# Layer 1 of a graph network: one head's product as an exponential of logs for eight row tiles in 32 instead of four, with adj added by GpSimd

## The chip, the cores and the metric

The kernel runs on one core of one Trainium2 chip. The metric is the device time of the whole program in microseconds. The kernel before took 2879.15 us (median of three runs, 2877.86 to 2881.1). In what follows TensorE is PE in the profile, VectorE is DVE, ScalarE is ACT, GpSimd is POOL and SyncE is SP; "us" is a microsecond.

## What is computed

The network has two layers over 4096 nodes with 512 features. Layer 0 (an attention with adj as mask) isn't touched. Layer 1, which the change touches, is a graph attention with 8 heads of 64 features; its connectivity is adj itself, added to the scores:

```python
data1 = (data @ W.T + b).reshape(N, H, D)            # N = 4096, H = 8, D = 64
src = jnp.einsum('nhd,xhd->nh', data1, src_proj)
trg = jnp.einsum('nhd,xhd->nh', data1, trg_proj)
e = src.T[:, :, None] + trg.T[:, None, :]
e = jnp.where(e >= 0, e, 0.01 * e)
e = e + connectivity[None, :, :]                     # adj, 0 or 1
scores = jax.nn.softmax(e, axis=-1)
out = jnp.einsum('hnm,hmd->hnd', scores, data1.transpose(1, 0, 2))
```

An unnormalised weight is thus exp(leaky(s + t)) times exp(adj). With the leaky slope 0.01, exp(leaky(s + t)) is the larger of two products of a factor of the column (from s) and one of the row (from t). The softmax is divided by its row sums at the end.

## The kernel before

**Layout.** Layer 1 holds the weights transposed: partitions are m (the neighbours, 32 row tiles of 128, NT = 32), the free dimension is n in blocks of WL = 1024 columns (two halves of BL = 512). A *group* i is one block of columns and one set of four heads, HG = 4: eight groups in all. A *step* is one row tile m of one group: 256 steps. For each step and each of the four heads k a tile pr of 128x1024 float32 is made, and TensorE multiplies it with the values.

**The stages.** The order of all work is written out by hand (line 1317 and the loop behind it): in step s each stage is called for the step that lies so many steps ahead, and each engine runs its instructions in the order in which they are issued.

- `load`, 4 ahead: SyncE loads the adj tile e (four buffers). At certain m it also loads the column factors z of the next group, and at m = 28 the column row u of the next group.
- `exps`, 1 ahead: ScalarE writes ex = exp(adj) into PSUM, one buffer (line 1061).
- `weigh`, 1 ahead: VectorE makes the products in the order 3, 0, 1, 2. Heads 1 and 2 (line 1107) and head 0 (line 1104) read ex from PSUM; head 3 (line 1107 too) reads e3 from SBUF. GpSimd adds product 3 onto the sum acc3 (line 1116) and, for the row tiles in BY_DMA, issues a DMA that adds product 0 onto one of two sums acc0 (line 1122).
- `factors`, 2 ahead: ScalarE writes e3 = exp(adj + log factor of the row) (line 1071), and for head 0 the Relu part rl (line 1089) from which VectorE's line 1104 makes the larger of the two products.
- `logs`, 0 ahead, before: see below.
- `scale`, 2 ahead, in the first two groups alone: GpSimd, later ScalarE (line 1057), scales the values by factors of the rows.
- `gather`, 0 ahead: TensorE's matmuls of the step (lines 1139 and 1144): 32 with the values and 8 for the row sums of heads 1 and 2. For a row tile that is not in BY_DMA TensorE also sums product 0 (line 1144 with zo). `side` counts these row tiles, and turns the order of the two halves of the array. At the last row tile the sums acc0 and acc3 are added up, and ScalarE copies the four results out of PSUM (line 1172).
- Behind the stages, at the steps in PARTS, a part of `finish` for the group before: transposes on TensorE, the reciprocal on VectorE, copies with a scale on ScalarE (line 1225), and a DMA that adds x on GpSimd's queue (line 1230). In group 0 this place belongs to `tables`.

**Head 0 by logs.** For the four row tiles in BY_LOG head 0's product takes another way, which needs no VectorE instruction: ScalarE makes lg = Relu of the column row u (line 1078), a DMA from GpSimd's queue adds adj from HBM onto it (line 1079), and ScalarE writes pr0 = exp(lg + log of the row) (line 1086). The dictionary says at which step lg is made: row tile 10 in step 5, 16 in 10, 22 in 16, 27 in 22. The exponential stands in `factors`, in place of that row's Relu of line 1089, and VectorE then has three products in the row's step. lg has one buffer, pr0 has three, the other products have two, rl two.

Of the kernel before, what the change touches and what calls it, by code (L numbers as in the profile page):

```python
# [8 lines left out]
FP = mybir.dt.float32  # L9
AF = mybir.ActivationFunctionType  # L10
ALU = mybir.AluOpType
# [4 lines left out]
P = 128  # L16
# [3 lines left out]
SLOPE = 0.01  # L20


def row_bcast(ap, n, offset=0):

    return bass.AP(tensor=ap.tensor, offset=ap.offset + offset, ap=[[0, P], [1, n]])
# [3 lines left out]
def kernel(  # L29
# [15 lines left out]
    nc = tc.nc  # L45
    N, F = x.shape
    H, D = 8, 64
    HG, WL = 4, 1024
    WT = WL // P
    NT = N // P  # L50
    KC = F // P
    BL = 512
# [12 lines left out]
    u_d = dram.tile([2, NT, P], FP, name="u_d")  # L65
# [20 lines left out]
    t_m = big.tile([P, H, NT], FP, name="t_m")  # L86
# [6 lines left out]
    rl = s_n.rearrange("p h t -> p (h t)").rearrange("p (t b) -> p t b", b=NB)  # L93
# [11 lines left out]
    with tc.tile_pool(name="w0", bufs=1) as wp, tc.tile_pool(name="a0", bufs=2) as ap_, tc.tile_pool(  # L105
        name="a0s", bufs=8
# [355 lines left out]
    with tc.tile_pool(name="mx", bufs=1) as mxp, tc.tile_pool(name="b_a", bufs=6) as adjp, tc.tile_pool(  # L462
        name="b_e", bufs=1
    ) as esp, tc.tile_pool(name="b_m", bufs=4) as mkp, tc.tile_pool(name="b_s", bufs=2) as sp, tc.tile_pool(
        name="b_p", bufs=6, space=PSUM
# [11 lines left out]
        def load(i, j, t):  # L477
            w, lo, sk = parts(i, j, t)
            rows = slice(t * P, (t + 1) * P)
            ar = adjp.tile([P, BL], FP, name="ar")  # L480
            nc.sync.dma_start(ar[:, :w], adj[rows, lo:lo + w])
            ac = adjp.tile([P, BL], FP, name="ac")
            nc.sync.dma_start(ac[:, :w], adj_t[rows, lo:lo + w])
            loaded[i, j, t] = ar, ac
# [36 lines left out]
        for n in range(-6, len(items)):  # L521
# [3 lines left out]
            if n >= 0:  # L525
                i, j, t = items[n]
# [17 lines left out]
    with tc.tile_pool(name="c_a", bufs=7) as adjp, tc.tile_pool(name="c_e", bufs=9) as etp, tc.tile_pool(  # L544
        name="c_d", bufs=5
    ) as wkp, tc.tile_pool(name="c_t", bufs=2) as atp, tc.tile_pool(name="c_u", bufs=2) as smp, tc.tile_pool(
        name="c_m", bufs=2
    ) as mxp, tc.tile_pool(name="c_o", bufs=4) as iop, tc.tile_pool(name="c_v", bufs=1) as cvp, tc.tile_pool(
        name="c_s", bufs=2
# [49 lines left out]
        def exps(b, m):  # L599
            if m == 0:  # L600
                mb = bank("m")
                nc.scalar.copy(mb, blk[b][0])
                blk[b][0] = mb
            mb, d, e, n = blk[b][0], ex[b, m], src.pop((b, m)), turned(b, m)
            if n:
                nc.vector.tensor_tensor(d[:, 0:n], d[:, 0:n], mb[:, 0:n], ALU.subtract)
            if n < BL:
                nc.vector.tensor_tensor(d[:, n:], e[:, n:], mb[:, n:], ALU.subtract)  # L608
            nc.scalar.activation(d, d, AF.Exp)  # L609
# [68 lines left out]
        left, scale, norms, joins = [], {}, iter(()), iter(())  # L678
# [191 lines left out]
        def gather(b, m):  # L870
# [5 lines left out]
            elif b:  # L876
                products(b - 1, NT // 2 - 1, PR[NF:])

        stages = ((load, 11), (load_a, 7), (gather, 0), (turn, 5), (exps, 4), (more_sums, 1), (weigh, 2), (sums, 2),
                  (residuals, 0))  # L880
        z = bank(PR[-1])
        pc = column_maxima(acc_z, z)
        dens = iter(())
        for s in range(-11, end):
            b, m = divmod(s, NT)
# [61 lines left out]
    nlg_m = l1.tile([P, H // HG, NT], FP, name="nlg_m")  # L947
# [26 lines left out]


    PARTS = (0, 1, 2, 3, 4, 6, 7, 8, 11, 12, 13, 18, 19, 20, 22)
    BY_LOG = {10: 5, 16: 10, 22: 16, 27: 22}
    BY_DMA = [m for m in range(NT) if m not in (4, 7, 13, 14, 19, 23, 24, 25, 29, 31)]

    with tc.tile_pool(name="p", bufs=2) as prp, tc.tile_pool(name="rl", bufs=2) as rlp, tc.tile_pool(  # L980
        name="io1", bufs=2
    ) as iop, tc.tile_pool(name="s1", bufs=1) as sp, tc.tile_pool(name="za", bufs=1) as zp0, tc.tile_pool(name="e3", bufs=2) as e3p, tc.tile_pool(
        name="zb", bufs=1
    ) as zp1, tc.tile_pool(name="e", bufs=4) as ep, tc.tile_pool(name="ac", bufs=2) as acp, tc.tile_pool(
        name="os", bufs=1
    ) as osp, tc.tile_pool(name="u", bufs=1) as usp, tc.tile_pool(
        name="p_x", bufs=1, space=PSUM
    ) as p_x, tc.tile_pool(name="p_v", bufs=1, space=PSUM) as p_v, tc.tile_pool(
        name="p_t1", bufs=1, space=PSUM
    ) as p_t, tc.manual_schedule():  # L990
        groups = [(b, g) for b in range(N // WL) for g in range(H // HG)]
        steps = [(i, m) for i in range(len(groups)) for m in range(NT)]
        us = {}
        zs_, ra, ex, e3, rl, pr, acc, pv, late = {}, {}, {}, {}, {}, {}, {}, {}, {}
# [35 lines left out]
        def zload(i, k):  # L1030
            b, g = groups[i]
            zs_[i, k] = (zp1 if i % 2 else zp0).tile([P, WL], FP, name=f"z{k}")
            nc.sync.dma_start(zs_[i, k], row_bcast(z_d, WL, (g * HG + k) * N + b * WL))

        def load(i, m):
            b, g = groups[i]
            e = ep.tile([P, WL], FP, name="e")
            nc.sync.dma_start(e, adj_t[m * P:(m + 1) * P, b * WL:(b + 1) * WL])
            ra[i, m] = e
            if i + 1 < len(groups) and m == 28:  # L1040
                us[i + 1] = usp.tile([P, WL], FP, name="u")
                b, g = groups[i + 1]
                nc.sync.dma_start(us[i + 1], row_bcast(u_d, WL, g * N + b * WL))
            m0, n = (3, 2) if i else (22, 1)
            if i + 1 < len(groups) and m0 <= m < m0 + HG // n:
                for k in ORDER[n * (m - m0):n * (m - m0) + n]:
                    zload(i + 1, k)

        def scale(i, m):


            if i < H // HG:
                for h in range(groups[i][1] * HG + 1, groups[i][1] * HG + 3):
                    if m < (6, 3)[i]:
                        nc.gpsimd.tensor_scalar(va[:, m, h, :], va[:, m, h, :], d_m[:, h, m:m + 1], None, ALU.mult)
                    else:
                        nc.scalar.activation(va[:, m, h, :], va[:, m, h, :], AF.Copy, scale=d_m[:, h, m:m + 1])

        def exps(i, m):
            x_ = p_x.tile([P, WL], FP, name="ex")  # L1060
            nc.scalar.activation(x_, ra.pop((i, m)), AF.Exp)  # L1061
            ex[i, m] = x_

        def factors(i, m):
            last_exps(i, m)
            relus(i, m)
# [4 lines left out]
            nc.scalar.activation(x_, ra[i, m], AF.Exp, bias=ld_m[:, h // HG, m:m + 1])  # L1071
            e3[i, m] = x_

        def logs(i, s):
            for m in [m for m in BY_LOG if BY_LOG[m] == s]:
                b, g = groups[i]
                r = rlp.tile([P, WL], FP, name="lg", bufs=1)
                nc.scalar.activation(r, us[i], AF.Relu, bias=nlg_m[:, g, m:m + 1], scale=-(1.0 - SLOPE))
                nc.gpsimd.dma_start(r, adj_t[m * P:(m + 1) * P, b * WL:(b + 1) * WL], accum_op=ALU.add)
                rl[i, m] = r  # L1080

        def relus(i, m):
            h = groups[i][1] * HG
            if m in BY_LOG:
                pr[i, m, 0] = prp.tile([P, WL], FP, name="pr0", bufs=3)
                nc.scalar.activation(pr[i, m, 0], rl.pop((i, m)), AF.Exp, bias=t_m[:, h, m:m + 1])
                return
            r = rlp.tile([P, WL], FP, name="rl")
            nc.scalar.activation(r, zs_[i, 0], AF.Relu, bias=ngd_m[:, h // HG, m:m + 1], scale=d_m[:, h, m:m + 1])  # L1089
            rl[i, m] = r  # L1090

        def weigh(i, m, order=ORDER):
            h = groups[i][1] * HG
            x_ = ex.pop((i, m))
            for k in order:
                if (i, m, k) in pr:
                    continue
                w = prp.tile([P, WL], FP, name=f"pr{k}", bufs=3 if k == 0 else 2)
                if k == 0 and (i, m) == (0, 0):
                    r = rlp.tile([P, WL], FP, name="rl")  # L1100
                    nc.vector.tensor_scalar(r, zs_[0, 0], g_m[:, 0, 0:1], d_m[:, 0, 0:1], ALU.max, ALU.mult)
                    nc.vector.tensor_tensor(w, r, x_, ALU.mult)
                elif k == 0:
                    nc.vector.scalar_tensor_tensor(w, rl.pop((i, m)), ngd_m[:, h // HG, m:m + 1], x_,  # L1104
                                                   op0=ALU.subtract, op1=ALU.mult)
                else:
                    nc.vector.scalar_tensor_tensor(w, zs_[i, k], g_m[:, h + k, m:m + 1],  # L1107
                                                   e3.pop((i, m)) if k == 3 else x_,
                                                   op0=ALU.max, op1=ALU.mult)
                pr[i, m, k] = w  # L1110
            w = pr[i, m, 3]
            if m == 1:
                acc[i, 3] = acp.tile([P, WL], FP, name="acc3", bufs=1)
                nc.gpsimd.tensor_tensor(acc[i, 3], pr[i, 0, 3], w, ALU.add)
            elif m > 1:
                nc.gpsimd.tensor_tensor(acc[i, 3], acc[i, 3], w, ALU.add)  # L1116
            if m == 1:
                for n in range(2):
                    acc[i, 0, n] = acp.tile([P, WL], FP, name=f"acc0{n}", bufs=1)
                    nc.gpsimd.dma_start(acc[i, 0, n], pr[i, n, 0])  # L1120
            elif m > 1 and m in BY_DMA:
                nc.gpsimd.dma_start(acc[i, 0, BY_DMA.index(m) % 2], pr[i, m, 0], accum_op=ALU.add)

        def gather(i, m):
            b, g = groups[i]
# [4 lines left out]
            v, dn = pv[i]  # L1130
            by_pe = [u for u in range(NT) if u not in BY_DMA]
            side = sum(u < m for u in by_pe) % 2
# [179 lines left out]
        weigh(0, 0, (3, 1, 2, 0))  # L1312
        scale(0, 0)
        factors(0, 1)
        scale(0, 1)

        stages = ((load, 4), (exps, 1), (weigh, 1), (factors, 2), (logs, 0), (scale, 2), (gather, 0))
        for s in range(len(steps)):
            for f, ahead in stages:
                if s + ahead < len(steps):  # L1320
# [47 lines left out]
```

## Time and profile before

The profiled execution took 2878.71 us. Its span, from the first to the last instruction, is 2876.9 us; the granted TensorE clock was 0.989.

| | us | share of the span |
|---|---|---|
| profiled execution | 2878.71 | |
| span | 2876.9 | |
| PE busy | 2770.8 | 96% |
| DVE busy | 2610.5 | 91% |
| ACT busy | 1391.4 | 48% |
| POOL busy | 1533.9 | 53% |
| HBM | 527.1 MB | 183 GB/s |

The page of the profile has the busy time of each engine, then the span in 40 slices with a digit of tenths, then groups of instructions. A group's line reads: source line, engine, operation, written and read tiles, shapes, count | busy time of the group, mean duration of one in ns | idle time of the engine just before these instructions and what ended it. A view in order of time has the start in us, the duration in us, the engine, the line and the tiles; `x2` is two instructions merged, and a bracket has the idle time before it and its releaser. A line of the waits has the waiting instruction, its releaser, the total in us, how often, and the longest. An instruction's duration is somewhat longer than the distance to the next start, as the engines overlap the end of one with the start of the next.

Layer 1's first product starts at 1671.0 us. The starts of the eight groups on VectorE (product 3 of row tile 0) are 1670.98, 1820.74, 1969.31, 2117.85, 2266.37, 2414.90, 2563.73 and 2712.25: 149.76 us for group 0 and 148.5 to 148.8 for the six behind it. The page's last groups of issues show the loads of e at 5.9 us from issue to landing (median), and the DMAs from product 0 to acc0 at 5.8.

### The profile page before, as it was taken

The page shows a single profiled execution, that of the slowest core. Times are in us where ns is not written, and L with a number is a line of the kernel's source. Part 1 is how long each engine was busy: PE and PEld are TensorE (multiplying, and loading weights), DVE is VectorE, ACT ScalarE, POOL GpSimd, SP SyncE. Part 2 cuts the span into 40 slices and gives each one's busy share as a digit, 9 for nine tenths or more (in the row PEclk, how much of TensorE's full clock was granted, in tenths as well). Part 3 has the DMA queues.
Part 4 walks back from the last instruction along what each step waited for, and adds up shares of the span by engine and source line. Part 5 has one row for each costly group of instructions (what it writes and reads, how often), then busy time and mean ns, then how long its engine had stood idle before and what let it go on. Part 6 is the DMA issues. An engine that isn't in the chain of part 4 may idle for free.

```text
span 2876.9 us, 47763 instructions
## 1 busy us (share of the span) xinstructions
PE 2770.8 (96%) x16859; PEld 1486.0 (52%) x16859; DVE 2610.5 (91%) x3694; ACT 1391.4 (48%) x2116; POOL 1533.9 (53%) x1320
## 2 busy tenths in 40 slices
PE   7999999997999999999998979999999999999998
PEld 4885444444888878878875424322222222222222
DVE  7877798898898898899995799999999999999998
ACT  2212233332223322322321078887878777878786
POOL 5323444443244345345454766676757675757675
PEclk9999999998999999999999989999999999999999
DMA  5538798887999876766754179898989898989896
GB/s 179 175 89 289 249 343 300 292 299 205 199 192 215 224 171 193 210 179 191 207 151 132 51 203 246 237 241 234 235 236 243 234 242 237 241 240 239 212 230 170
DMA packets 528321, 622.60 MB, mean 216 GB/s; under 512 B 294136, under 2 KB 346392, under 8 KB 528080
## 3 DMA queue, kind: packets, MB, share of 16 engines
q1 hardware_dynamic: 461488, 413.00, 48.4%
q0 software_dynamic: 64576, 202.61, 29.8%
q10 hardware_dynamic: 2016, 3.93, 0.4%
q8 instruction: 132, 2.16, 0.3%
q14 instruction: 109, 0.89, 0.1%
HBM read 421.01 MB, written 106.10 MB: 183 GB/s over the span
## 4 chain that ended last, share of the span: by engine, by line
PE 70%; DVE 16%; DMA 6%; issue 5%; ACT 2%; SPq 1%; DVEq 0%; POOL 0%; ACTq 0%; POOLq 0%
PE pv L1139 26%; PE pe L501 14%; PE po L669 11%; PE dn L1144 8%; PE bank L269 6%; PE po L809 4%; DVE pr L1107 4%; DVE at L616 3%; DMA et<-er_d 2%; DVE d L608 2%; DVE u L637 1%; DMA a<-in_adj_t_dram 1%; SPq L581 1%; ACT e L1071 1%; DMA et<-ec_d 1%
## 5 line engine op out<-in xcount | busy, mean ns | idle before, releaser
L1139 PE MATMUL pv<-pr,sup 128*32 128x512 f32 x8192 | 1020.7, 594 | 14.0 <-DMA e<-in_adj_t_dram 10.9
L1116 POOL TENSOR_TENSOR acc<-acc,pr 128x1024 f32<-128x1024 f32 x240 | 572.8, 2387 | 311.5 <-DVE pr L1107 309.8
L1107 DVE SCALAR_TENSOR_TENSOR pr<-z,g_m,ex 128x1024 f32<-128x1024 f32 x512 | 630.1, 1270 | 0.0
L1139 PEld LDWEIGHTS pv<-pr,sup 128*32 128x32 f32 x8192 | 294.0, 110 | 608.7 <-issue 564.7
L609 ACT ACTIVATE d<-d 128x512 f32<-128x512 f32 x256 | 161.1, 630 | 542.1 <-DVE d L608 321.4
L501 PE MATMUL pe<-he_t,he_t 128*128 128x512 f32 x896 | 386.4, 592 | 0.0
L1061 ACT ACTIVATE ex<-e 128x1024 f32<-128x1024 f32 x256 | 263.3, 1028 | 241.7 <-DVE pr L1107 239.2
L1144 PE MATMUL dn<-pr,d_m 128*2 128x512 f32 x1984 | 344.7, 592 | 0.0
L1107 DVE SCALAR_TENSOR_TENSOR pr<-z,g_m,e 128x1024 f32<-128x1024 f32 x256 | 327.3, 1279 | 0.0
L1071 ACT ACTIVATE e<-e,ld_m 128x1024 f32<-128x1024 f32 x256 | 290.7, 1135 | 0.0
L1104 DVE SCALAR_TENSOR_TENSOR pr<-rl,ngd_m,ex 128x1024 f32<-128x1024 f32 x223 | 283.2, 1270 | 1.9 <-ACT ex L1061 1.6
L501 PEld LDWEIGHTS pe<-he_t,he_t 128*128 128x128 f32 x896 | 169.2, 190 | 208.4 <-issue 192.6
L1089 ACT ACTIVATE rl<-z,ngd_m,d_m 128x1024 f32<-128x1024 f32 x223 | 273.8, 1228 | 0.0
L616 DVE TENSOR_TENSOR at<-d,a 128x512 f32<-128x512 f32 x256 | 215.4, 842 | 54.7 <-PE po L669 44.7
L669 PE MATMUL po<-he_t,at 128*128 128x256 f32 x1024 | 263.9, 380 | 0.0
L669 PE MATMUL po<-sup,u 128*128 128x256 f32 x1024 | 262.8, 379 | 0.0
L669 PE MATMUL po<-sup,at 128*128 128x256 f32 x1024 | 244.3, 381 | 13.4 <-DVE at L616 13.4
L622 POOL TENSOR_TENSOR racc<-racc,d 128x512 f32<-128x512 f32 (+2 forms) x136 | 181.0, 1331 | 96.5 <-ACT d L609 91.3
L669 PEld LDWEIGHTS po<-sup,at 128*128 128x128 f32 x1024 | 195.3, 191 | 41.3 <-DVE at L616 14.7
L669 PEld LDWEIGHTS po<-sup,u 128*128 128x128 f32 x1024 | 194.7, 190 | 26.6
L669 PEld LDWEIGHTS po<-he_t,at 128*128 128x128 f32 x1024 | 193.5, 190 | 28.1 <-DVE sc L689 2.3
L506 POOL DMA_DIRECT2D er_d<-mk x136 | 74.4, 547 | 234.8 <-DVE rm L503 227.0
(261 smaller groups left out, 3748.7 us busy)
## 6 DMA issues: line engine op xcount, KB each, us to landing
e<-in_adj_t_dram SPq DMA_DIRECT2D x256, 512.0 KB, 5.9
acc<-pr POOLq DMA_DIRECT2D x176, 512.0 KB, 5.8
a<-in_adj_t_dram SPq DMA_DIRECT2D x256, 256.0 KB, 3.6
ar<-in_adj_dram SPq DMA_DIRECT2D x120, 256.0 KB, 4.8
ac<-in_adj_t_dram SPq DMA_DIRECT2D x120, 256.0 KB, 5.1
ec_d<-mc POOLq DMA_DIRECT2D x120, 256.0 KB, 4.8
et<-ec_d SPq DMA_DIRECT2D x120, 256.0 KB, 3.5
er_d<-mk POOLq DMA_DIRECT2D x112, 256.0 KB, 4.2
```

The costliest lines, as they stand in the source:

```text
L501: nc.tensor.matmul(pe[:, :w], he_t[i][:, k, (t % TB) * P:(t % TB + 1) * P], he_t[j][:, k, BL - w:], start=(k == 0), stop=(k == KC - 1))
L616: nc.vector.tensor_tensor(w[:, m % 2, :], d, aj.pop((b, m)), ALU.mult)
L622: nc.gpsimd.tensor_tensor(racc[:, c0:], racc[:, c0:], d[:, c0:], ALU.add)
L669: nc.tensor.matmul(acc[:, j, :], A[:, j * P:(j + 1) * P], B, start=(first_ and j == 0), stop=last, skip_group_check=True)
L1061: nc.scalar.activation(x_, ra.pop((i, m)), AF.Exp)
L1071: nc.scalar.activation(x_, ra[i, m], AF.Exp, bias=ld_m[:, h // HG, m:m + 1])
L1089: nc.scalar.activation(r, zs_[i, 0], AF.Relu, bias=ngd_m[:, h // HG, m:m + 1], scale=d_m[:, h, m:m + 1])
L1104: nc.vector.scalar_tensor_tensor(w, rl.pop((i, m)), ngd_m[:, h // HG, m:m + 1], x_, op0=ALU.subtract, op1=ALU.mult)
L1107: nc.vector.scalar_tensor_tensor(w, zs_[i, k], g_m[:, h + k, m:m + 1], e3.pop((i, m)) if k == 3 else x_, op0=ALU.max, op1=ALU.mult)
L1116: nc.gpsimd.tensor_tensor(acc[i, 3], acc[i, 3], w, ALU.add)
L1139: nc.tensor.matmul(v[c][q][r * D + c0:r * D + c0 + Q, :], va[:, m, g * HG + k, c0:c0 + Q], pr[i, m, k][:, q * BL:(q + 1) * BL], start=(m = ...
L1144: nc.tensor.matmul(dn[r * Q:r * Q + w.shape[1], :], w, src[:, q * BL:(q + 1) * BL], **fl)
```

## The change

Eight row tiles of a group go by logs instead of four. lg is made four steps ahead (`logs` is now 4 ahead, at a fixed distance). adj isn't fetched again from HBM: GpSimd adds it from the tile e in SBUF, in two instructions of 512 columns, the first half after the sum of line 1116 two row tiles earlier, the second after that of the row tile before. The exponential moves from `factors` to `exps`, behind the row's own ex. The row u of a group is loaded with the group's first e instead of at m = 28 of the group before. BY_DMA has 23 row tiles instead of 22, so TensorE sums product 0 of nine row tiles instead of ten, and the alternation of the two sums acc0 is turned so that the last DMA still goes to the second.

```diff
-    BY_LOG = {10: 5, 16: 10, 22: 16, 27: 22}
-    BY_DMA = [m for m in range(NT) if m not in (4, 7, 13, 14, 19, 23, 24, 25, 29, 31)]
+    BY_LOG = (3, 6, 11, 16, 20, 25, 28, 31)
+    BY_DMA = [m for m in range(NT) if m not in (5, 8, 10, 14, 18, 22, 24, 29, 31)]
...
-            if i + 1 < len(groups) and m == 28:
-                us[i + 1] = usp.tile([P, WL], FP, name="u")
-                b, g = groups[i + 1]
-                nc.sync.dma_start(us[i + 1], row_bcast(u_d, WL, g * N + b * WL))
+            if i and m == 0:
+                us[i] = usp.tile([P, WL], FP, name="u")
+                nc.sync.dma_start(us[i], row_bcast(u_d, WL, g * N + b * WL))
...
             nc.scalar.activation(x_, ra.pop((i, m)), AF.Exp)
             ex[i, m] = x_
+            if m in BY_LOG:
+                h = groups[i][1] * HG
+                pr[i, m, 0] = prp.tile([P, WL], FP, name="pr0", bufs=3)
+                nc.scalar.activation(pr[i, m, 0], rl.pop((i, m)), AF.Exp, bias=t_m[:, h, m:m + 1])
...
-        def logs(i, s):
-            for m in [m for m in BY_LOG if BY_LOG[m] == s]:
-                b, g = groups[i]
+        def logs(i, m):
+            if m in BY_LOG:
                 r = rlp.tile([P, WL], FP, name="lg", bufs=1)
-                nc.scalar.activation(r, us[i], AF.Relu, bias=nlg_m[:, g, m:m + 1], scale=-(1.0 - SLOPE))
-                nc.gpsimd.dma_start(r, adj_t[m * P:(m + 1) * P, b * WL:(b + 1) * WL], accum_op=ALU.add)
+                nc.scalar.activation(r, us[i], AF.Relu, bias=nlg_m[:, groups[i][1], m:m + 1], scale=-(1.0 - SLOPE))
                 rl[i, m] = r
+
+        def add_logs(i, m, half):
+            if m in BY_LOG:
+                cs = slice(half * BL, (half + 1) * BL)
+                nc.gpsimd.tensor_tensor(rl[i, m][:, cs], rl[i, m][:, cs], ra[i, m][:, cs], ALU.add)
 
         def relus(i, m):
             h = groups[i][1] * HG
             if m in BY_LOG:
-                pr[i, m, 0] = prp.tile([P, WL], FP, name="pr0", bufs=3)
-                nc.scalar.activation(pr[i, m, 0], rl.pop((i, m)), AF.Exp, bias=t_m[:, h, m:m + 1])
                 return
...
                 nc.gpsimd.tensor_tensor(acc[i, 3], acc[i, 3], w, ALU.add)
+            add_logs(i, m + 1, 1)
+            add_logs(i, m + 2, 0)
...
-                nc.gpsimd.dma_start(acc[i, 0, BY_DMA.index(m) % 2], pr[i, m, 0], accum_op=ALU.add)
+                nc.gpsimd.dma_start(acc[i, 0, (len(BY_DMA) + BY_DMA.index(m)) % 2], pr[i, m, 0], accum_op=ALU.add)
...
         factors(0, 1)
+        logs(0, 3)
         scale(0, 1)
 
-        stages = ((load, 4), (exps, 1), (weigh, 1), (factors, 2), (logs, 0), (scale, 2), (gather, 0))
+        stages = ((load, 4), (exps, 1), (weigh, 1), (factors, 2), (logs, 4), (scale, 2), (gather, 0))
```

## The prediction

> **What bounds the kernel now.** I read the page first, then the waits of layer 1, then the rows in order of time of VectorE, ScalarE, GpSimd and TensorE. The change touches only layer 1, from 1671 us to the end.
>
> ```profile
> DVE  7877798898898898899995799999999999999998
> L1104 DVE SCALAR_TENSOR_TENSOR pr<-rl,ngd_m,ex 128x1024 f32<-128x1024 f32 x223 | 283.2, 1270 | 1.9 <-ACT ex L1061 1.6
> L1089 ACT ACTIVATE rl<-z,ngd_m,d_m 128x1024 f32<-128x1024 f32 x223 | 273.8, 1228 | 0.0
> L1061 ACT ACTIVATE ex<-e 128x1024 f32<-128x1024 f32 x256 | 263.3, 1028 | 241.7 <-DVE pr L1107 239.2
> ```
>
> VectorE is full through layer 1 and hardly ever waits. ScalarE idles, and its idle time lies before one instruction, the exponential ex: that writes the one PSUM buffer ex and so must wait until VectorE's last product of the step before has read it. The waits say the same, and name the reverse wait, which is rare:
>
> ```profile
> ACT ex L1061 <- DVE pr L1107: 236.1, 229, 1.6
> DVE pr L1104 <- ACT ex L1061: 1.6, 8, 0.3
> ```
>
> The rows in order of time give the length of a step. In group 2, around row tile 10, by logs in the kernel before:
>
> ```profile
> 2014.82 1.14 ACT L1086 ACTIVATE pr<-lg,t_m 128x1024 f32<-128x1024 f32 x1
> 2017.58 1.03 ACT L1061 ACTIVATE ex<-e 128x1024 f32<-128x1024 f32 x1 [0.82 <-DVE pr L1107]
> 2018.55 1.13 ACT L1071 ACTIVATE e<-e,ld_m 128x1024 f32<-128x1024 f32 x1
> 2019.59 1.23 ACT L1089 ACTIVATE rl<-z,ngd_m,d_m 128x1024 f32<-128x1024 f32 x1
> 2021.16 1.03 ACT L1061 ACTIVATE ex<-e 128x1024 f32<-128x1024 f32 x1 [0.34 <-DVE pr L1107]
> ...
> 2017.47 1.28 DVE L1107 SCALAR_TENSOR_TENSOR pr<-z,g_m,e 128x1024 f32<-128x1024 f32 x1
> 2018.66 2.47 DVE L1107 SCALAR_TENSOR_TENSOR pr<-z,g_m,ex 128x1024 f32<-128x1024 f32 x2
> 2021.05 1.32 DVE L1107 SCALAR_TENSOR_TENSOR pr<-z,g_m,e 128x1024 f32<-128x1024 f32 x1
> 2022.29 1.27 DVE L1104 SCALAR_TENSOR_TENSOR pr<-rl,ngd_m,ex 128x1024 f32<-128x1024 f32 x1
> ```
>
> VectorE's products follow each other at 1.19 us: 4.77 us for a step of four, 3.58 us (2017.47 to 2021.05) for a step by logs, which has three. Starts on ScalarE are 0.965 us apart after an ex, 1.04 after the exponential of line 1071, 1.14 after a Relu of line 1089, and 1.04 after the two operations of a log row (lines 1078 and 1086: 1703.74 to 1704.78, 2014.82 to 2015.86). In this log step ScalarE had 0.965 + 1.04 + 1.14 = 3.145 us to do and waited 0.34: the log row's own exponential (2014.82) had run a step ahead.
>
> Where ScalarE has more to do than VectorE's step lasts, VectorE waits. The end of a group shows it, where the four copies of line 1172 come on top:
>
> ```profile
> 2121.10 2.02 ACT L1172 COPY os<-pv 128x512 f32<-128x512 f32 x4
> 2122.99 1.05 ACT L1061 ACTIVATE ex<-e 128x1024 f32<-128x1024 f32 x1
> ...
> 2122.63 1.27 DVE L1107 SCALAR_TENSOR_TENSOR pr<-z,g_m,e 128x1024 f32<-128x1024 f32 x1
> 2124.08 1.28 DVE L1104 SCALAR_TENSOR_TENSOR pr<-rl,ngd_m,ex 128x1024 f32<-128x1024 f32 x1 [0.18 <-ACT ex L1061]
> ```
>
> From ex at 2117.96 to ex at 2122.99 are 5.03 us, 3.145 + 1.89, and the following VectorE step took 5.04 instead of 4.77. So a step lasts as long as the longer of VectorE's products and ScalarE's work between two ex: that is the rule of my sum. A group of 32 steps took 148.52 us: 28 x 4.77 + 4 x 3.58 = 147.9, 0.27 for these copies, 0.27 for the reciprocal, the rest in steps behind log rows. TensorE has almost no room either: its slots of four concurrent matmuls follow at 0.4287 us, 10 a step (4.29). With row 0's sums and the turning I count 336 slots = 144.0 us, 4 us of transposes and 0.2 of waiting: 148.2 a group.
>
> **The change, part by part.** *VectorE loses* one product in four more row tiles: 4 x 1.19 = 4.77 us a group, 38 in all, if nothing else fills the place.
>
> *TensorE* sums eight of the row tiles' products besides the last instead of nine. A lone one that is closed by a transpose costs two slots, a pair also two. Before: 4; 7; (13,14); (19,23); (24,25). After: 5; (8,10); (14,18); (22,24). Two slots, 0.86 us a group. Floor after: about 147.4.
>
> *ScalarE, the dear part.* A log row's exponential moves from `factors` (a step ahead, where it replaced a Relu of 1.14) to `exps`, right behind its own ex. It then stands in VectorE's short step, and ahead of e3 and the Relu of the next row, and of the next ex. ScalarE's work in that step is 0.965 + 1.04 + 1.04 + 1.14 = 4.185 us against 3.58. Besides, the Relu of `logs` (1.04) now stands four steps ahead: for rows 6, 28 and 31 it falls into the step of the log rows 3, 25 and 28, 5.225 us. Row 20's step also has four copies of `finish` (0.85): 5.035. The steps by logs: 3 x 5.225 + 4 x 4.185 + 5.035 = 37.45, where VectorE alone would need 28.6. The Relu falls on busy steps elsewhere too: row 3's on the copies at the group's end (3.145 + 1.04 + 1.89 = 6.075), rows 11's and 16's on `finish` copies in steps 8 and 13 (5.035 each). The other 21 steps stay at 4.77: 100.2; the reciprocal hides under row 3's step.
>
> *GpSimd* gets two adds of 512 columns for each log row and loses four DMA issues of 0.87 a group (one more accumulating DMA). No row of layer 1 has this shape; those of line 820 (128x512) take 1.27 us, those of line 163 up to 1.82. I take 1.27, the operands being alike. After the sum of line 1116 (start 1.44 us into the step, next start 2.33 later) a half ends at 5.04 us, 0.27 into the next step; the log row's exponential wants it 1.08 in. So the halves are mostly in time. One is not: in step 9 GpSimd has sum, half, DMA issue and then the 1.49 us issue of `finish`, so row 10's sum starts 1 us late and row 11's second half meets VectorE's product 3. That product and GpSimd's sum do meet in this trace:
>
> ```profile
> 2464.77 2.39 POOL L1116 TENSOR_TENSOR acc<-acc,pr 128x1024 f32<-128x1024 f32 x1 [0.64 <-DVE pr L1107]
> 2466.63 1.61 DVE L1107 SCALAR_TENSOR_TENSOR pr<-z,g_m,e 128x1024 f32<-128x1024 f32 x1
> 2468.16 1.27 DVE L1104 SCALAR_TENSOR_TENSOR pr<-rl,ngd_m,ex 128x1024 f32<-128x1024 f32 x1
> ```
>
> Product 3, the one with both inputs in SBUF, lasts 0.33 us longer than 1.28; it gets going 0.2 us before GpSimd's end, as it does at 2021.05, where it lost 0.04. For row 11 I bound the loss by 0.3 (half first) and 1.4 (product first, ScalarE waits for the half) and take 0.9, in the middle. An ordinary first half costs its next product 0.07; five of them lie in steps of 4.77: 0.35 a group. With halves of 1.82 us it would be 0.6 each, 3 a group: the upper end. No gain is possible from an added wait, so the lower end is zero.
>
> The Trainium skill, "SBUF — State Buffer", section "Who interferes with whom", says that a VectorE instruction with two SBUF inputs and a GpSimd one that reads SBUF exclude each other for the whole instruction. The two rows agree, but for the last 0.2 us. By the rule taken fully an ordinary half would cost 0.27, and the sum would be 8 us more.
>
> *DMA and SyncE.* The four adding DMAs a group (8.1 to 11.4 us to landing) go. The load of u moves to the next group's first load, step 28 of the group before; it waits for row 31's Relu, and lands (9.4 us) some 7 us before row 3's Relu needs it. The e load behind it in SyncE's queue waits for an ex of about that time anyway. I put both at nothing; a late u would hold ScalarE, and so the ex, by its lateness.
>
> **Sum.** Groups 2 to 6: 37.45 + 0.9 + 6.075 + 10.07 + 100.2 + 0.35 = 155.0, which is 6.5 more than 148.52; five groups, 32.5. Group 1 has two more ScalarE copies a step (line 1057, 0.48): six log steps, steps 8 and 13 grow by that, row 20's too: 159.3, +10.8. Group 0 has these and the tables, but no `finish`: 156.4 against 149.76, +6.6. Group 7: its last log step has no next rows, +5.9. In all +55.8. The profiled execution took 2878.71 us (span 2876.9, 1.8 around it), the median of the runs is 2879.15, 0.4 above: 2878.7 + 55.8 = 2934.5.
>
> **The case's own range.** Without the GpSimd terms +45; with 1.4 for row 11 and long halves +79: 2924 to 2958.
>
> **Rivals.** *Faster: TensorE is the bound.* If ScalarE's extra work in log steps were covered, VectorE would need 144 us a group and TensorE 147.4 to 147.7: 0.86 to 1.1 less, 7 to 9 us, 2871. For it: TensorE's rows leave no gap now, and ScalarE is busy under 80%. Against: one ex buffer, and the 5.04 us step above; an average share doesn't help a queue in order. 8%.
>
> *No change.* If the eight steps cost only the plain 4.185 and the Relus and `finish` copies found gaps, a group would be 24 x 4.77 + 8 x 4.185 + 0.5 = 148.5: 2879. Against: they stand in the same queue ahead of the next ex. 7%.
>
> *Slower by GpSimd.* It falls behind for good: it has 2.33 + 0.6 to 0.9 a step and 1.27 more in half the steps, up to 4.5 us of 4.85; if its lateness carries on, product 3 and the log exponential meet it in every pair of log steps, 0.5 to 1 us in 16 steps a group: 2960 to 3000. It decides from a half of about 1.7 us on. 9%.
>
> That the logs aren't made by the new way: nothing in the diff allows it. 2% for what I have not seen.
>
> **Numbers.** My case has 74%. The range takes it in and reaches towards both sides: 2906 to 2962. Under 0.2% (5.8 us) a measurement here can't tell from no change. Slower 85% (74 + 9 + 2), same 6%, faster 9%, the seven for no change lying across that border.
>
> **What would show it.** ScalarE's idle time before ex falls, and VectorE's before lines 1104 and 1107, released by ex, rises from 1.6 us to some 90. The step of rows 25 and 28 lasts 5.2 us, of 6 and 16 4.2. Line 1104 has 191 instructions, lines 1078 and the moved exponential 64 each, 128 half adds at 1.27. TensorE gets gaps. It is wrong if log steps still last 3.6 us, or if VectorE's waits name GpSimd or a DMA.

## The result, and the profile after

The changed kernel took 2927.86 us (median of four runs, 2926.1 to 2928.9); the kernel before, on the same chip, 2880.12. The ratio is 1.0166, with a 95% interval of 1.0148 to 1.0183: 48 us slower, where 55.8 had been forecast. The profiled execution took 2926.1 us, 47.4 more than that of before. Its groups start on VectorE 156.9, 157.7, 154.1, 153.8, 153.8, 153.8 and 153.8 us apart; before it was 149.8 and then 148.5 to 148.8.

The page of the changed kernel, the lines that answer to those shown of before (line 1108 was 1104, 1111 was 1107, 1060 was 1061). The first line is of the kernel before, for product 3:

```profile
L1107 DVE SCALAR_TENSOR_TENSOR pr<-z,g_m,e 128x1024 f32<-128x1024 f32 x256 | 327.3, 1279 | 0.0
...
DVE  7867798888898899889986799999999999999997
L1060 ACT ACTIVATE ex<-e 128x1024 f32<-128x1024 f32 x256 | 262.2, 1024 | 268.2 <-DVE pr L1111 266.3
L1111 DVE SCALAR_TENSOR_TENSOR pr<-z,g_m,e 128x1024 f32<-128x1024 f32 x256 | 348.1, 1360 | 0.0
L1108 DVE SCALAR_TENSOR_TENSOR pr<-rl,ngd_m,ex 128x1024 f32<-128x1024 f32 x191 | 243.7, 1276 | 61.5 <-ACT ex L1060 60.3
```

The slices can't show it: in tenths VectorE looks as full as before. The idle column does. The wait of product 0 for ex has risen from 1.6 to 60.3 us, in 64 places of 1.9 us at most. Product 3's group has also grown from 327.3 to 348.1 us with the same 256 instructions: these 21 us are waits too, spent inside an instruction, which the page counts as busy (e2_no_adds below shows that 17 of them go with GpSimd's adds). VectorE has lost 32 instructions of 1.19 us and gained some 80 us of waiting.

Row 25 of group 2 of the changed kernel in order of time: ScalarE from the ex of row 24 on, VectorE from product 3 of row 25 on; the other engines are left out:

```profile
2101.37 1.03 ACT L1060 ACTIVATE ex<-e 128x1024 f32<-128x1024 f32 x1 [1.54 <-DVE pr L1111]
2102.34 1.14 ACT L1074 ACTIVATE e<-e,ld_m 128x1024 f32<-128x1024 f32 x1
2106.13 1.36 DVE L1111 SCALAR_TENSOR_TENSOR pr<-z,g_m,e 128x1024 f32<-128x1024 f32 x1
2106.24 1.03 ACT L1060 ACTIVATE ex<-e 128x1024 f32<-128x1024 f32 x1 [2.76 <-DVE pr L1111]
2107.20 1.13 ACT L1065 ACTIVATE pr<-lg,t_m 128x1024 f32<-128x1024 f32 x1
2107.41 2.46 DVE L1111 SCALAR_TENSOR_TENSOR pr<-z,g_m,ex 128x1024 f32<-128x1024 f32 x2
2108.24 1.13 ACT L1074 ACTIVATE e<-e,ld_m 128x1024 f32<-128x1024 f32 x1
2109.28 1.23 ACT L1093 ACTIVATE rl<-z,ngd_m,d_m 128x1024 f32<-128x1024 f32 x1
2109.79 1.32 DVE L1111 SCALAR_TENSOR_TENSOR pr<-z,g_m,e 128x1024 f32<-128x1024 f32 x1
2110.42 1.13 ACT L1080 ACTIVATE lg<-u,nlg_m 128x1024 f32<-128x1024 f32 x1
2111.46 1.00 ACT L1060 ACTIVATE ex<-e 128x1024 f32<-128x1024 f32 x1
2112.49 1.28 DVE L1108 SCALAR_TENSOR_TENSOR pr<-rl,ngd_m,ex 128x1024 f32<-128x1024 f32 x1 [1.38 <-ACT ex L1060]
```

From one ex to the next, five instructions of ScalarE stand back to back (ex itself, then lines 1065, 1074, 1093 and 1080): 5.22 us. VectorE is through with the log row at 2109.79 and does product 3 of the next row; product 0 then waits 1.38 us for the ex that ScalarE hasn't come to. ScalarE itself had waited 2.76 us just before: in the step ahead it had two instructions only, as the log row's own Relu is not needed. The work is there, in the wrong step.

### The profile page after: what moved, and what is told of

It is laid out like the page before. It is cut to its first block, busy times and chain, and to the rows that moved or that the text cites. A ratio compares the mean times of both kernels' runs of the same rounds, so it can differ in the third digit from the quotient of the medians.

```text
span 2924.3 us, 47837 instructions
## 1 busy us (share of the span) xinstructions
PE 2782.1 (95%) x16827; PEld 1476.5 (50%) x16827; DVE 2599.9 (89%) x3662; ACT 1415.1 (48%) x2148; POOL 1669.2 (57%) x1424
## 4 chain that ended last, share of the span: by engine, by line
PE 50%; DVE 22%; ACT 13%; DMA 6%; issue 6%; SPq 1%; POOL 0%; DVEq 0%; ACTq 0%; POOLq 0%
PE pe L501 14%; PE po L669 12%; PE pv L1145 10%; DVE pr L1111 9%; PE bank L269 6%; ACT e L1074 4%; PE po L809 4%; PE dn L1150 3%; DVE at L616 3%; DMA et<-er_d 2%; ACT rl L1093 2%; ACT ex L1060 2%; ACT pr L1065 2%; DVE d L608 2%; DVE pr L1108 1%
## 5 line engine op out<-in xcount | busy, mean ns | idle before, releaser
L1145 PEld LDWEIGHTS pv<-pr,sup 128*32 128x32 f32 x8192 | 281.7, 110 | 662.3 <-issue 498.0
L1060 ACT ACTIVATE ex<-e 128x1024 f32<-128x1024 f32 x256 | 262.2, 1024 | 268.2 <-DVE pr L1111 266.3
L1111 DVE SCALAR_TENSOR_TENSOR pr<-z,g_m,e 128x1024 f32<-128x1024 f32 x256 | 348.1, 1360 | 0.0
L1150 PE MATMUL dn<-pr,d_m 128*2 128x512 f32 x1984 | 328.7, 592 | 0.0
L1108 DVE SCALAR_TENSOR_TENSOR pr<-rl,ngd_m,ex 128x1024 f32<-128x1024 f32 x191 | 243.7, 1276 | 61.5 <-ACT ex L1060 60.3
L1093 ACT ACTIVATE rl<-z,ngd_m,d_m 128x1024 f32<-128x1024 f32 x191 | 234.8, 1229 | 0.0
```

Of the source, the lines that this page charges most:

```text
L1145: nc.tensor.matmul(v[c][q][r * D + c0:r * D + c0 + Q, :], va[:, m, g * HG + k, c0:c0 + Q], pr[i, m, k][:, q * BL:(q + 1) * BL], start=(m = ...
L1150: nc.tensor.matmul(dn[r * Q:r * Q + w.shape[1], :], w, src[:, q * BL:(q + 1) * BL], **fl)
```

## The experiments

They ran in four sets, each against the kernel before on the same chip (2880 us, 2879.8 to 2880.9 in the four sets); differences between sets are taken from what each run lost or gained against the kernel before of its own set. The steps given are distances from ex to ex in groups 2 to 7, if nothing else is said.

**e4_moved: the kernel before, with one part of the change.**

```diff
 # exps
             ex[i, m] = x_
+            if m in BY_LOG:
+                h = groups[i][1] * HG
+                pr[i, m, 0] = prp.tile([P, WL], FP, name="pr0", bufs=3)
+                nc.scalar.activation(pr[i, m, 0], rl.pop((i, m)), AF.Exp, bias=t_m[:, h, m:m + 1])
 # relus
             if m in BY_LOG:
-                pr[i, m, 0] = prp.tile([P, WL], FP, name="pr0", bufs=3)
-                nc.scalar.activation(pr[i, m, 0], rl.pop((i, m)), AF.Exp, bias=t_m[:, h, m:m + 1])
                 return
```

> The kernel before with one part of the change alone: the log row's exponential moves from `factors` to `exps`, behind its row's ex. Still four log rows, adj still added by DMA, no add on GpSimd. Theory (ScalarE's queue): the four log steps grow from 3.58 to 4.18, and by 0.48 more in groups 0 and 1: 2.4 a group, 23 in all: 2899 to 2905 us. Rival (GpSimd): no add is there, so no change, 2880 within 4. Rival (TensorE is the bound, and VectorE's and ScalarE's delays are swallowed by its lag): no change either.

2897.62 us, ratio 1.0059 (1.0044 to 1.0074). Each log step went from 3.58 to 4.18 us, 4.65 in groups 0 and 1, with no add on GpSimd. The time is 1.4 us below the range that was expected, and the loss is 17 us instead of 23: the step behind a log row is 4.74 instead of 4.81, 2 us in all; the rest was not followed up. The place of one ScalarE instruction costs 17 us here by itself.

**e2_no_adds: the changed kernel without GpSimd's adds** (the line of `tensor_tensor` in `add_logs` becomes `pass`).

> The changed kernel without GpSimd's half adds: adj is left out of head 0's exponent in the eight log row tiles of each group; all else is as it was. Theory (ScalarE's queue): only what the adds cost by meeting product 3 goes, 0.2 in row 11, 0.04 behind it and 0.1 in rows 19, 24 and some others, 0.5 a group: 2922 to 2926 us. Rival (GpSimd): nearly all of the 48 us goes: 2880 to 2890.

2923.09 us, ratio 1.0145 (1.0128 to 1.0162). Row 11's step fell from 4.39 to 4.18, and rows 19 and 24 from 4.88 to 4.77. The adds are worth some 5 us of the 48, so the rest isn't theirs. From its page:

```profile
L1111 DVE SCALAR_TENSOR_TENSOR pr<-z,g_m,e 128x1024 f32<-128x1024 f32 x256 | 331.3, 1294 | 0.0
L1108 DVE SCALAR_TENSOR_TENSOR pr<-rl,ngd_m,ex 128x1024 f32<-128x1024 f32 x191 | 244.0, 1278 | 73.1 <-ACT ex L1060 71.9
```

Without the adds product 3 takes 17 us less than in the changed kernel, but product 0 waits 12 us longer for ex. So most of what VectorE waits for GpSimd in the changed kernel is time in which it would otherwise wait for ScalarE; what is left over is the 5 us.

**e3_spaced: other log rows, the same eight.**

```diff
-    BY_LOG = (3, 6, 11, 16, 20, 25, 28, 31)
+    BY_LOG = (3, 7, 11, 15, 19, 23, 27, 31)
```

> The changed kernel with the log row tiles (3, 7, 11, 15, 19, 23, 27, 31): again eight, with the same instructions, but never three apart, so that no Relu of `logs` falls into a log row's step, and none in the step of row 20. Theory (ScalarE's queue): eight log steps of 4.18, the group's first of 6.06, three of 4.96, twenty of 4.77, and about 0.6 for the adds that come late: 150.4 a group instead of 153.8: 2898 to 2904 us. Rival (GpSimd): as many adds in as many steps, 2928 within 5.

2904.39 us, ratio 1.0082 (1.0067 to 1.0097), 0.4 us above the range that was expected. No log step is longer than 4.18, but for rows 11 and 23 at 4.4, where GpSimd's late half decides, and row 7 in one group (4.32). The Relu of `logs` in log steps, and the copies in row 20's, were about half of the loss.

**e9_relu_moved: the changed kernel with the next row's Relu in the empty place.**

```diff
         def relus(i, m):
             h = groups[i][1] * HG
-            if m in BY_LOG:
+            if m - 1 in BY_LOG:
                 return
+            if m in BY_LOG:
+                m += 1
+                if m == NT:
+                    return
```

> The changed kernel with one edit: the Relu of line 1093 for the row behind a log row is made a step earlier, in the place that the log row's own Relu leaves empty (it needs only z and two factors). Exponential, adds, rows and counts stay. Theory (ScalarE's queue): between two ex a log step then holds 3.045 us instead of 4.185, 4.085 with the Relu of `logs` and 3.83 with the `finish` copies: rows 3, 25, 28 fall from 5.2 to 4.1 us, 6 and 16 from 4.2 to 3.6, 20 from 4.96 to 3.85, 31 to 3.6; row 11 stays at 4.4, where GpSimd's late half decides. Group 0.0 to 0.8 above 148.5: 2880 to 2890 us. Rival (GpSimd's adds, once log steps are short again, meet product 3 as in e1_early): above 2900.

2885.91 us, ratio 1.0023 (1.0014 to 1.0033): 42 of the 48 us are back, by moving one ScalarE instruction of 1.14 us by one step, behind seven of a group's eight log rows (row 31 has no next row in its group). Row 25 of group 2, ScalarE in order of time, to be laid beside the same row above:

```profile
2091.04 1.03 ACT L1060 ACTIVATE ex<-e 128x1024 f32<-128x1024 f32 x1 [1.63 <-DVE pr L1115]
2092.00 1.13 ACT L1065 ACTIVATE pr<-lg,t_m 128x1024 f32<-128x1024 f32 x1
2093.04 1.14 ACT L1074 ACTIVATE e<-e,ld_m 128x1024 f32<-128x1024 f32 x1
2094.08 1.13 ACT L1080 ACTIVATE lg<-u,nlg_m 128x1024 f32<-128x1024 f32 x1
2095.12 1.00 ACT L1060 ACTIVATE ex<-e 128x1024 f32<-128x1024 f32 x1
```

4.08 us from ex to ex, 1.14 less, and ScalarE's wait ahead of it has shrunk by the same 1.13. Rows 6 and 16 take 3.68: there VectorE's three products set the step, with 0.1 lost to a half add.

**e1_early: the exponential a step ahead again, a miss.**

```diff
 # exps: the log row's exponential is taken out; relus: it is put back, as in e4_moved reversed
 # ahead of the loop over the steps, logs(0, 3) is called earlier
-            add_logs(i, m + 1, 1)
-            add_logs(i, m + 2, 0)
+            add_logs(i, m + 2, 1)
+            add_logs(i, m + 3, 0)
-        stages = ((load, 4), (exps, 1), (weigh, 1), (factors, 2), (logs, 4), (scale, 2), (gather, 0))
+        stages = ((load, 4), (exps, 1), (weigh, 1), (factors, 2), (logs, 5), (scale, 2), (gather, 0))
```

> The changed kernel with the log row's exponential back in `factors`, a step ahead, and so the Relu of `logs` five steps ahead and the two half adds a row tile earlier; the row tiles and all counts of instructions stay. Theory (ScalarE's queue: what it has to do between two ex sets the step): rows 6, 11, 25 and 28 fall from 4.2 to 5.2 us to 3.6; row 16 stays near 4.2, since row 20's Relu now falls into its step, and row 31 too by row 3's; a group needs about 145.5 us of VectorE and ScalarE, so TensorE's 147.4 bounds: 2866 to 2880 us. If product 0's three buffers, written a step earlier, hold ScalarE up, it is some us more. Rival (GpSimd's adds and the SBUF reads it shares with VectorE): the same 128 adds, so it stays within 10 us of 2928.

2929.6 us, ratio 1.0171 (1.0156 to 1.0187), as slow as the change and where the rival had put it. The log steps did fall as the theory had it: 6, 11, 25 and 28 to 3.58, 16 and 31 to 4.18. But rows 27 and 30 took 6.7 us, and row 4 up to 8.5. GpSimd, VectorE and ScalarE behind log row 28 of group 3, from product 3 of row 29 to product 0 of row 30, show how, lines 1082 and 1118 being the half add and the sum, 1109 product 3 (the products with ex and ScalarE's other rows are left out):

```profile
2278.60 1.33 DVE L1109 SCALAR_TENSOR_TENSOR pr<-z,g_m,e 128x1024 f32<-128x1024 f32 x1
2278.81 2.27 POOL L1082 TENSOR_TENSOR lg<-lg,e 128x512 f32<-128x512 f32 x1
2281.03 0.84 POOL L1126 DMA_DIRECT2D acc<-pr  x1
2281.64 2.65 POOL L1118 TENSOR_TENSOR acc<-acc,pr 128x1024 f32<-128x1024 f32 x1
2283.42 3.20 DVE L1109 SCALAR_TENSOR_TENSOR pr<-z,g_m,e 128x1024 f32<-128x1024 f32 x1
2283.98 1.55 POOL L1082 TENSOR_TENSOR lg<-lg,e 128x512 f32<-128x512 f32 x1
2286.54 1.27 DVE L1106 SCALAR_TENSOR_TENSOR pr<-rl,ngd_m,ex 128x1024 f32<-128x1024 f32 x1
2287.23 1.15 ACT L1088 ACTIVATE pr<-lg,t_m 128x1024 f32<-128x1024 f32 x1 [1.60 <-DMA acc<-pr]
```

The half add stands behind the sum of log row 28, whose step lasts only 3.58 us. It comes 3.8 us after that step's start, meets the next product 3, and takes 2.27 us instead of 1.27; the DMA issue and the sum behind it are late; the sum and the next half together then keep the following product 3 from 2283.42 to 2286.54; and product 0's buffer, which the late DMA still reads, holds up the exponential of row 31 for 1.60. Rows 25 to 27 of the same group repeat this pattern, with the same 2.27 and 3.20. (Row 4 has besides a half add waiting for its tile e.)

**e5_early_no_adds: e1_early without the adds** (again `pass` in `add_logs`).

> The run e1_early, in which the exponential stands a step ahead again and which stayed at 2930, without GpSimd's half adds: adj is left out of head 0's exponent in the eight log row tiles. It tells apart why e1_early kept its loss. Theory A (the adds: with log steps short again, a first half behind a log row's sum meets the next product 3, and GpSimd's sum and half in a row keep that product back by 2 to 3.4 us; the accumulating DMA behind the half is late too): the long steps 2, 4, 27 and 30 (5.1 to 8.5 us) fall to about 4.8, a group needs about 146 us, TensorE's floor of 147.4 bounds: 2868 to 2880 us. Theory B (product 0's three buffers alone: the exponential written a step earlier waits for TensorE or the DMA of three rows before): steps 27 and 30 keep 6.7, 2905 us or more.

2870.54 us, ratio 0.9969 (0.9958 to 0.9980). Theory A holds: rows 27 and 30 are at 4.77, and the time is at the floor that TensorE's slots give: groups 1 to 6 take 147.45 us on average, and in each TensorE has 0.25 us between its matmuls. From the page:

```profile
L1106 DVE SCALAR_TENSOR_TENSOR pr<-rl,ngd_m,ex 128x1024 f32<-128x1024 f32 x191 | 243.2, 1273 | 14.3 <-ACT ex L1060 13.5
L1109 DVE SCALAR_TENSOR_TENSOR pr<-z,g_m,e 128x1024 f32<-128x1024 f32 x256 | 329.8, 1288 | 0.0
```

Product 3 is back at 1288 ns from 1535 in e1_early. So the adds that cost 5 us in the changed kernel (e2_no_adds) cost 58 in e1_early: what they cost is decided by where they stand. ScalarE's lateness alone did not keep them cheap in the changed kernel: e9_relu_moved has the adds where the change has them, most of its log steps are short again, and it is 6 us slower than the kernel before, not 49. What differs in e1_early is that a half add stands behind a log row's own sum.

**e6_seven and e8_eight: the exponential early, rows at least four apart, misses both.**

```diff
 # exponential and half adds as in e1_early; e8 has the rows that its expectation names
-    BY_LOG = (3, 6, 11, 16, 20, 25, 28, 31)
-    BY_DMA = [m for m in range(NT) if m not in (5, 8, 10, 14, 18, 22, 24, 29, 31)]
+    BY_LOG = (6, 10, 15, 19, 23, 27, 31)
+    BY_DMA = [m for m in range(NT) if m not in (3, 7, 12, 16, 20, 24, 28, 31)]
...
+        stages = ((load, 4), (exps, 1), (logs, 4), (weigh, 1), (factors, 2), (scale, 2), (gather, 0))
```

> A version by the theory of both queues: seven log row tiles (6, 10, 15, 19, 23, 27, 31), at least four apart; exponential a step ahead, in `factors`; the half adds in the two row tiles before that, so that none stands in a log row's step; the Relu of `logs` right behind ex, four steps ahead, so that it falls in no log step; TensorE sums product 0 of the rows three before a log row (3, 7, 12, 16, 20, 24, 28) and of 31, so that the buffer is free without a DMA. VectorE and ScalarE: 25 x 4.77 + 7 x 3.62 + 0.2 + 0.3 + 14 x 0.1 for the halves = 146.5 a group; TensorE 334 slots, about 147.4 to 147.6. So 148.5 falls to 147.5 and the time to 2870 to 2876 us. Rival (GpSimd's adds cost in any place): above 2885.

> As e6_seven with eight log row tiles (3, 7, 11, 15, 19, 23, 27, 31), four apart, and TensorE's sums in rows 4, 8, 12, 16, 20, 24, 28 and 31. Row 3's Relu falls on the copies at the group's end (6.06), those of rows 7, 11 and 23 on `finish` copies (4.96). VectorE and ScalarE: 24 x 4.77 + 8 x 3.62 + 1.3 + 0.6 + 1.6 + 0.3 = 147.3 a group, level with TensorE: 2872 to 2884 us. Rival (GpSimd): slower than e6_seven by 1/7 of what adds cost, above 2890.

2901.13 us (ratio 1.0073, 1.0061 to 1.0086) and 2904.24 (1.0086, 1.0073 to 1.0100): both times lie where the rivals had put them. The waits of e6_seven name what the sum had left out:

```profile
POOL lg L1082 <- DMA e<-in_adj_t_dram: 49.3, 23, 6.1
ACT pr L1088 <- POOL lg L1082: 20.4, 7, 3.8
```

The first half add, a row earlier than in the change, asks for its tile e before that has landed (87.4 us of such waits in e8_eight), and then comes late into product 3: steps of 5.8 to 7 us in rows 9, 14, 18, 26 and 28 of many groups. It isn't a price of the add as such, as the rivals had it: e11_seven_placed below has the same seven log rows and as many adds, and takes 2872.1 us.

**e10_placed: the exponential where the change has it, e9's Relu, and rows by hand.**

```diff
 # on top of e9_relu_moved; ahead of the loop over the steps logs(0, 2) in place of logs(0, 3)
+    BY_LOG = (2, 6, 10, 15, 18, 22, 26, 30)
+    BY_DMA = [m for m in range(NT) if m not in (5, 9, 14, 21, 31)]
```

> e9_relu_moved with the log row tiles (2, 6, 10, 15, 18, 22, 26, 30) and TensorE's sums in rows 5, 9, 14, 21 and 31 alone (BY_DMA has 27). Three or more apart, no half add in a log row's step; the Relu of `logs` off the copies at the group's end and of `finish`, in a log step only once (18's in row 15's, 4.1 us); no accumulating DMA on GpSimd in the rows where `finish` issues its own. VectorE and ScalarE: 24 x 4.77 + 8 x 3.62 + 0.5 + 0.3 + 0.3 + 1.6 for the halves + 0.6 for late ones = 146.7 a group; TensorE 332 slots, 146.5. So 1.8 us a group less than before: 2862 to 2872 us. Rival (GpSimd's adds meet product 3): above 2885.

2884.91 us, ratio 1.0016 (1.0007 to 1.0025): 13 us above the range, and at the rival's border. Every step was as planned but row 0 at 5.5 and row 4 at 7.2 to 7.8 us. GpSimd and VectorE there, in group 4 (line 1130 issues the two DMAs that fill acc0, 1132 the accumulating DMA, 1124 is the sum):

```profile
2285.64 1.14 POOL L1130 DMA_DIRECT2D acc<-pr  x2
...
2293.19 0.88 POOL L1132 DMA_DIRECT2D acc<-pr  x1 [3.94 <-DVE pr L1115]
2293.83 2.67 POOL L1124 TENSOR_TENSOR acc<-acc,pr 128x1024 f32<-128x1024 f32 x1
2294.12 3.47 DVE L1115 SCALAR_TENSOR_TENSOR pr<-z,g_m,e 128x1024 f32<-128x1024 f32 x1
2297.51 1.27 DVE L1112 SCALAR_TENSOR_TENSOR pr<-rl,ngd_m,ex 128x1024 f32<-128x1024 f32 x1
```

The issue names a VectorE product as its releaser, but row 2's product comes from ScalarE, and was done at 2287.6. What it waited for is in the trace: the second of the two DMAs that fill acc0, onto which this one adds, landed at 2292.65, and in each of the eight groups the issue starts 0.54 to 0.55 us after that landing. The sum that came late then kept product 3 of row 4 back, as the rival had it, though in one row; row 0 is the other place where a half add met product 3.

**e11_seven_placed and e12_eight_placed: that reading put to the test, in two ways.**

```diff
 # e11: on top of e10, no log row ahead of 6, and so without logs(0, 2)
+    BY_LOG = (6, 10, 15, 19, 23, 27, 31)
 # e12: on top of e10, row 2's product summed by TensorE
+    BY_DMA = [m for m in range(NT) if m not in (2, 5, 9, 14, 21, 31)]
```

> e10_placed with seven log row tiles (6, 10, 15, 19, 23, 27, 31). In e10_placed every step was as planned but two: row 0 took 5.5 us, as row 2's first half waited for its Relu and met product 3, and row 4 took 7.2 to 7.8 where 4.8 was planned: GpSimd stood 3.9 us at row 2's accumulating DMA, issued so soon behind the two DMAs that fill acc0 that these hadn't landed, and the sum that came late kept product 3 of row 4 back. With no log row ahead of 6 both should go: rows 0 to 5 at 5.03, 4.77, 4.77, 4.77, 4.95, 4.9. VectorE and ScalarE about 146.5 a group, TensorE 332 slots, 146.5 to 146.9: 1.6 us a group less than before: 2865 to 2872 us. Rival (the eight adds cost by themselves wherever they stand): above 2878.

> e10_placed with row 2's product 0 summed by TensorE (rows 2, 5, 9, 14, 21, 31) and so no accumulating DMA in row 2; still eight log rows with row 2 among them. By the same reading row 4's 7.2 us falls to about 4.9, and row 0 keeps 5.5: VectorE and ScalarE 146.1 a group; TensorE has two slots more, 334 or 147.4, and bounds: 2868 to 2876 us. If row 4 keeps 7 us, the DMA was not its cause.

2872.1 us (ratio 0.9970, 0.9959 to 0.9982) and 2871.56 (0.9972, 0.9962 to 0.9983). In e12_eight_placed row 4 fell to 4.95 with the DMA of row 2 gone: the DMA was its cause. Both compute the whole result and are 8 us faster than the kernel before, 56 less than the change. e12_eight_placed has the eight log rows and 128 half adds of the change; TensorE sums product 0 of six row tiles instead of nine, and three more go by DMA. e11_seven_placed has one log row less. From the page of e11_seven_placed:

```profile
L1060 ACT ACTIVATE ex<-e 128x1024 f32<-128x1024 f32 x256 | 263.7, 1030 | 211.0 <-DVE pr L1115 207.7 <-DVE pr L1110 2.2
L1112 DVE SCALAR_TENSOR_TENSOR pr<-rl,ngd_m,ex 128x1024 f32<-128x1024 f32 x199 | 253.0, 1271 | 4.6 <-ACT ex L1060 4.2
```

The wait of product 0 for ex is at 4.2 us, from 60.3.

## Why the prediction was right, point by point

**The rule of the sum.** A step lasts as long as the longer of VectorE's products and ScalarE's work between two ex. It held in the log steps but for row 11: rows 3, 25 and 28 at 5.22 us (5.225 had been worked out), 6, 16 and 31 at 4.18 (4.185); and in row 0 at 6.06 (6.075). e4_moved shows it with one instruction, e9_relu_moved from the other side. The rival of no change needed gaps for the Relus of `logs`; rows 3, 25 and 28 show that they found none.

**Row 11 was mis-sized.** It took 4.39 us in groups 2 to 7, not 5.085: GpSimd's late half costs 0.2, not 0.9. The prediction had two ways in which the half and product 3 could meet and took the middle. In the changed kernel, row 11 of group 2 (lines 1120 and 1086 are the sum and the half add):

```profile
2036.42 3.08 POOL L1120 TENSOR_TENSOR acc<-acc,pr 128x1024 f32<-128x1024 f32 x1
2038.77 1.96 POOL L1086 TENSOR_TENSOR lg<-lg,e 128x512 f32<-128x512 f32 x1
2039.76 2.07 DVE L1111 SCALAR_TENSOR_TENSOR pr<-z,g_m,e 128x1024 f32<-128x1024 f32 x1
```

The half went first and kept product 3 back by 0.8; but VectorE has 0.6 to spare in a log step of 4.18, and so 0.2 came through. This is 0.7 in six groups, and 0.9 in group 1, where nothing came through: 5 of the 8 us between forecast and result. Some 1.5 us more are the `finish` copies, 0.78 instead of 0.85 in three steps of a group. The result lies near the lower end of the case's own range (2924 to 2958), whose upper end rested on half adds of 1.82 us; 121 of the 128 lasted under 1.5.

**GpSimd.** A half add took 1.26 us at its shortest, 1.28 in the median, as taken from line 820. An ordinary half cost its product 3 0.1 us, against the 0.07 of the sum. The rival that was slower by GpSimd didn't come about in the change. But e1_early, with the same 128 adds a row tile earlier and the exponential a step earlier, lost 58 us by them: the prediction asked whether GpSimd falls behind, where the question was which of its instructions stands in the row of a short step.

**The rival that was faster.** TensorE's floor of about 147.4 us a group is where e5_early_no_adds ends (2870.5, forecast for this rival 2871). It was ruled out for the right reason: ScalarE was 77% busy in the changed kernel (115.0 of the 150 us from 2300 to 2450) and still late.

**What would show it.** Three of these signs were not rightly worked out. VectorE's wait for ex rose to 60 us, not some 90: a further 21 are inside product 3, and, as e2_no_adds shows, stand mostly in place of a wait for ex. ScalarE's idle time before ex did not fall but rose, from 241.7 to 268.2 us: the kernel lasts 47 us longer, and ScalarE has only 24 us more to do (1391.4 to 1415.1). What fell is the wait before the next ex of a log step, which in row 25 is gone. And VectorE's waits could not have named GpSimd, since this wait stands in the profile as part of an instruction. TensorE waits for VectorE's products, as expected: its weight loads wait 86.0 us for line 1111, from 22.6 for line 1107.

## What to carry to other kernels

Where two engines hand one buffer back and forth, a step costs the longer of their two queues between two handovers; count each queue step by step, since a mean share of 77% hides a queue that is full in one step and empty in the one before. An instruction that needs nothing of the current step (here a Relu of row factors) belongs into the emptiest step, and that can be worth more than the instruction that was saved. Work added to an engine with room to spare is cheap only where it doesn't stand behind other work in a step that has just become shorter.

## What the runs showed of the hardware

A VectorE product with both inputs in SBUF and a two-input add on GpSimd keep each other out, both ways. In the rows shown, the product that comes second gets going about 0.2 us before GpSimd's end (worked out as its own end less 1.28 us); a half add that comes second took 2.27 us instead of 1.27. And two GpSimd adds in a row both went ahead of a waiting product: in e1_early it stood from 2283.42 until the second one's end at 2285.53 and was done 1 us later. The products with ex, which is in PSUM, kept 1.27 us (1.26 to 1.28 for all 512 in e1_early) with the adds about. The time lost so stands in the profile as a longer instruction and not as idle time.
